# Late parts of the last attention block moved in a hand-written order, ahead of the first state-space block's norms, lengths and parameters

## The chip, the cores and the metric

One of the cores of one Trainium2 chip runs the whole network in one launch. The core has TensorE (PE in the profile; its weight loads are PEld), VectorE (DVE), ScalarE (ACT), GpSimd (POOL) and SyncE (SP), which here only issues DMAs. Each engine works through its own queue of instructions, and the queues wait for each other by semaphores. The metric is the device time of one execution, in microseconds, lower being better.

## The reference

The input `x` has 64 sequences of 64 positions with 256 channels; `cond` has 512 numbers for each sequence. Four layers follow, each added to its input:

```python
x = x + attention(x, cond)      # layer 0: 16 heads, width 256
x = x + attention(x, cond)      # layer 1
x = x + state_space(x, cond)    # layer 2: inner width 512, state 16
x = x + state_space(x, cond)    # layer 3

# attention: styled layer norm, then
q, k, v = (xn @ Wq.T) * q_dc, (xn @ Wk.T) * k_dc, (xn @ Wv.T) * v_dc * s2
out = softmax(q @ k.T * scale) @ v
return (out @ Ww.T) * w_dc + (v @ Wu.T) * u_dc

# state space: a gated recurrence over the 64 positions
xr, gate = split(x @ W_in.T);  xr = xr + cond
xc = silu(causal_conv4(xr) + b_conv)
xn = layernorm(xc) * ln_g + ln_b
Bm, Cm, dt = split(xn @ W_xproj.T)
dt = tanh(dt @ W_dt.T + b_dt) * 0.01
Ad = 1 - dt * tanh(A_log);  Bd = Bm * min(norm(xn), 1)
for t in range(64):
    h = clip(h * Ad[t] + Bd[t] * xn[t], -10, 10)
    y[t] = Cm[t] @ h + D * xn[t]
return (y * silu(gate)) @ W_out.T
```

All arithmetic is in float32.

## The kernel before

The activations stay in SBUF in one tile `xt`, channels on the partitions, from the first load to the last store. An attention block (`Att`) is 8 sequences, 512 columns, of one layer; there are 8 blocks for each of the two layers, 16 in all, so the last has index 15 and its tiles carry the name `1_7`. A state-space block (`Block`) is 32 sequences by 16 time steps of one layer; `b0`, `b1` and `b2` are the first three, all of layer 2 and of the same 32 sequences.

Each block is a set of small methods ("parts"), and each part issues a few instructions on one to three engines. The order of the parts is written by hand: a list of events with a due time each, which is sorted and then issued. An attention block's parts have times relative to its index (`att_plan`), so the parts of block 15 are due at 15 plus the table's number. The parts of `b0`, `b1` and `b2` that run beside the last attention block have absolute times, such as 15.63. Since almost all instructions are pinned to the order in which they are issued, a due time sets the place of a part in the queue of every engine that it uses. After the last event the loop over the time steps begins, and its order is another table.

These are the parts that matter, with the names that their tiles have in the profile.

Of the last attention block:

- `soft_a(g)`, `soft_b(g)` for four groups g: row maxima `mx` and subtraction `pr` on DVE, the exponential of `pr` on ACT, then sums `sm` on DVE and the product of `pr` with them on POOL (L816).
- `turn(g)`: PE transposes `pr` in two halves `pt`, and ACT copies each to `pT` (L830).
- `attend(g)`: PE multiplies `pT` with the values into `po`, for two groups at a time; `collect(h)`: ACT copies `po` to `oT` (L851).
- `out(3, oc)`: PE projects `oT` (`pw`), DVE scales it into `t` (L123).
- `add`: POOL adds the residual `xt` to the other projection, `t` (L865, 128x1024).
- `leave`: the sum goes back to `xt`; in the last block alone DVE adds one half (L123, `xt<-t,t`) and POOL the other (L880).

Of the state-space blocks:

- `project(c)`, `collect(c)` for four channel groups c: PE computes `acc`, DVE or ACT and POOL put it into the window `xr` (for `b0`, `b1` and the first group of `b2` it is one DVE addition, L123). `collect(0)` of a block first copies the halo of the block before (L195). All blocks use one `xr` buffer.
- `begin(c)` on ACT and `taps(c, 1, 2, 3)` on DVE (L117, `acc_s`): the first and the other three products of the convolution. The last tap of the last group is followed by the copy of the halo on POOL (L234).
- `silu(c)`: ACT, to `xc`.
- `turn_x(j)` for four row groups j: PE transposes `xc` to `ptr`; `stats(j)`: DVE computes mean and variance and the centred, scaled `xg`, POOL the inverse root `rs` (L301, L302). There are two `xg` buffers.
- `norm(j)`: ACT multiplies `xg` by `rs`, POOL adds the offset to give `xn` (L318).
- `length(j)`: ACT squares `xn` and sums (it writes over `xg`).
- `flip`, `flipped`: PE transposes the small projections to `pxt`, ACT copies them to `pt` (L277).
- `params`, `strength`, `by_step`, `spread_b`, `decay`, `spreads`: small POOL instructions on `pt` (L329 to L407, L348), with one ACT tanh; the last of them are `exa` and `exc` (L336).
- `turn_a`, `turned_a`, `turn_c`, `turned_c`: PE turns `exa` and `exc` to `pa` and `pc`, ACT copies them to `ad` and `cd`. POOL has cleared `cd` before (L975).
- The loop: for each time step PE computes the input product `pu`, DVE the clipped state `h` in two halves (L1069 at the first step, L1072 later), ACT the decayed state `v`, PE the output `py`.

PSUM tiles of the attention phase (`ptr`, `pt`, `pxt`, `acc`, `pw`) take turns in three buffers.

Of the kernel before, what the change touches and what calls it, by code (L numbers as in the profile page):

```python
# [60 lines left out]
def tile_kernel(ctx: ExitStack, tc: tile.TileContext, ins, out):  # L61
# [520 lines left out]
    with tc.tile_pool(name="xpool", bufs=1) as xpool, tc.tile_pool(  # L582
# [318 lines left out]
        ablocks = [Att(n) for n in range(len(atts))]  # L901
# [9 lines left out]
        b0, b1, b2 = blocks[0], blocks[1], blocks[2]  # L911
        events = []

        def at(when, *parts):
            events.extend((when, b, part, args) for b, part, *args in parts)

        for n, b in enumerate(ablocks):
            for when, *part in att_plan:
                at(n + when, (b, *part))

        for when, k in ((-0.83, 4), (-0.7, 4), (-0.45, 4), (0.05, 4), (0.7, 4)):
# [22 lines left out]
        at(15.38, *((b0, "silu", c) for c in range(IC)))  # L944
        at(15.409, (b0, "shared"), (b0, "keep"))
        at(15.47, (b0, "flip"), (b0, "flipped"))
        for j, when in enumerate((15.446, 15.49, 15.54, 15.624)):
            at(when, (b0, "turn_x", j), (b0, "stats", j), (b0, "norm", j, True), (b0, "length", j))
        at(15.61, (b1, "begin", 0), (b1, "begin", 1))
        at(15.63, (b0, "params"), (b0, "strength"), (b0, "by_step"), (b0, "spread_b", 0),  # L950
           (plan0, None), (b0, "decay"), (b0, "spreads"))
        at(15.64, (b1, "taps", 0, 1, 2, 3))
        at(15.8, (b1, "begin", 2), (b1, "begin", 3), (b1, "taps", 1, 1, 2, 3))
        at(15.9, (b1, "taps", 2, 1, 2, 3))
        at(16.071, (b2, "project", 0))
        at(16.1, (b1, "taps", 3, 1, 2, 3), (b2, "collect", 0))
# [9 lines left out]
    with tc.tile_pool(name="m1", bufs=1) as m1, tc.tile_pool(  # L966
# [95 lines left out]
        for n, blk in enumerate(blocks):  # L1062
            for t in range(BT):
                j, t4 = divmod(t, T4)
                hs = []
                for h in range(2):
# [3 lines left out]
                    else:  # L1070
                        pin(
                            nc.vector._custom_dve(  # L1072
                                TENSOR_ADD_SAT, out=hn, in0=vs[h], in1=pus[h], s0=10.0, s1=-10.0
# [107 lines left out]
```

## Time and profile before

| | us |
|---|---|
| runs shown (median; lowest to highest) | 1637.25; 1634.78 to 1639.84 |
| profiled execution, its own time | 1634.85 |
| its span | 1633.1 |
| around the span | 1.75 |
| first state update of the loop (DVE h L1069) begins | 579.62 into the span |

The profile is one execution of the program. Its page gives busy times for each engine, the span in 40 slices and the chain of work that ended last. A timeline lists an engine's instructions in order of time: start, duration, engine, line, operation, tiles (written `out<-in`), shapes, count, and in brackets the idle time ahead of it and what ended it. The granted TensorE clock was 0.99 over the span and lower in the stretch where attention hands over to the state-space layers (0.71 from 544 to 576).

### The profile page before, as it was taken

The page shows a single profiled execution, that of the slowest core. Times are in us where ns is not written, and L with a number is a line of the kernel's source. Part 1 is how long each engine was busy: PE and PEld are TensorE (multiplying, and loading weights), DVE is VectorE, ACT ScalarE, POOL GpSimd, SP SyncE. Part 2 cuts the span into 40 slices and gives each one's busy share as a digit, 9 for nine tenths or more (in the row PEclk, how much of TensorE's full clock was granted, in tenths as well). Part 3 has the DMA queues.
Part 4 walks back from the last instruction along what each step waited for, and adds up shares of the span by engine and source line. Part 5 has one row for each costly group of instructions (what it writes and reads, how often), then busy time and mean ns, then how long its engine had stood idle before and what let it go on. Part 6 is the DMA issues. An engine that isn't in the chain of part 4 may idle for free.

```text
span 1633.1 us, 30221 instructions
## 1 busy us (share of the span) xinstructions
PE 1541.5 (94%) x12352; PEld 640.1 (39%) x12352; DVE 1308.7 (80%) x1480; ACT 1117.4 (68%) x1899; POOL 867.3 (53%) x862
## 2 busy tenths in 40 slices
PE   5899999999999688999999999999999999999888
PEld 2555555555555322333333333333333333333223
DVE  3776777677776677998989888988898889888775
ACT  3555554454466467887878888878788887787774
POOL 2467566566666755365455464554554545635410
PEclk9999999999999799999999999999999999999999
DMA  7000000000000010000000000000000000000001
GB/s 236 2 1 2 2 2 2 2 2 2 2 2 2 1 62 1 1 1 1 1 1 1 1 1 1 1 1 1 1 8 7 14 1 14 14 1 14 14 1 27
DMA packets 19339, 18.27 MB, mean 11 GB/s; under 512 B 5473, under 2 KB 16353, under 8 KB 19201
## 3 DMA queue, kind: packets, MB, share of 16 engines
q1 hardware_dynamic: 19200, 16.34, 3.2%
q8 instruction: 98, 1.61, 0.4%
q14 instruction: 41, 0.33, 0.1%
HBM read 12.14 MB, written 4.19 MB: 10 GB/s over the span
## 4 chain that ended last, share of the span: by engine, by line
PE 73%; DVE 13%; ACT 8%; issue 3%; POOL 2%; DMA 1%; SPq 0%; DVEq 0%; POOLq 0%; ACTq 0%
PE pw L107 24%; PE pu L107 14%; DVE h L1072 11%; PE py L107 8%; ACT v L113 6%; PE acc L107 6%; PE pt L110 4%; PE pg L107 3%; PE pv L107 3%; PE ps L107 2%; PE po L107 2%; PE mx L107 2%; PE ptr L110 2%; POOL xr L204 1%; PE pm L107 1%
## 5 line engine op out<-in xcount | busy, mean ns | idle before, releaser
L113 ACT ACTIVATE v<-h,ad 128x512 f32<-128x512 f32 x1008 | 651.1, 710 | 116.0 <-DVE h L1072 111.3
L1072 DVE CUSTOM_DVE_ANT_0 h<-v,pu 128x1024 f32<-128x1024 f32 x504 | 593.1, 1217 | 126.4 <-PE pu L107 64.3
L107 PE MATMUL pu<-xn,bd 32*128 32x512 f32 x2048 | 293.7, 641 | 41.3 <-DVE h L1072 39.5
L204 POOL TENSOR_TENSOR xr<-xr,cT 128x512 f32<-128x512 f32 x55 | 70.3, 1278 | 401.4 <-ACT xr L203 401.4
L107 PE MATMUL py<-h,cd 128*32 128x512 f32 x2048 | 276.2, 610 | 0.5 <-DVE h L1072 0.4
L107 PE MATMUL pw<-xm,aw 128*128 128x512 f32 x384 | 179.9, 607 | 3.9 <-POOL xm L724 3.9
L107 PEld LDWEIGHTS pu<-xn,bd 32*128 32x128 f32 x2048 | 83.3, 183 | 210.7 <-issue 142.3
L816 POOL TENSOR_TENSOR pr<-pr,sm 128x1024 f32<-128x1024 f32 x64 | 121.1, 1902 | 21.9 <-DVE sm L815 20.4
L107 PE MATMUL pg<-xt,win 128*128 128x512 f32 x256 | 129.3, 607 | 2.9 <-ACT ad L113 2.9
L117 DVE SCALAR_TENSOR_TENSOR acc<-xr,cv,acc 128x512 f32<-128x512 f32 x165 | 123.9, 751 | 3.5 <-ACT acc L113 1.6
L107 PE MATMUL acc<-xt,win 128*128 128x512 f32 x256 | 123.8, 607 | 0.0
L830 ACT COPY pT<-pt 128x512 f32<-128x512 f32 x128 | 68.4, 586 | 76.1 <-PE pt L110 76.1
L107 PE MATMUL pw<-z,wo 128*128 128x512 f32 x240 | 119.0, 618 | 0.0
L107 PEld LDWEIGHTS py<-h,cd 128*32 128x32 f32 x2048 | 40.5, 108 | 196.9 <-issue 157.1
L113 ACT ACTIVATE pr<-pr 128x1024 f32<-128x1024 f32 x64 | 67.7, 1057 | 61.1 <-DVE pr L123 61.1
L107 PEld LDWEIGHTS pw<-xm,aw 128*128 128x128 f32 x384 | 69.0, 191 | 74.0 <-issue 65.3
L113 ACT ACTIVATE acc<-xr,cv 128x512 f32<-128x512 f32 x55 | 43.0, 782 | 77.3 <-POOL xr L204 77.3
L434 POOL TENSOR_TENSOR dx<-xn,rep 128x512 f32<-128x512 f32 x64 | 82.0, 1281 | 26.2 <-DVE ys L123 26.2
L805 DVE TENSOR_REDUCE mx<-ps 128x16 f32<-128x1024 f32 x64 | 78.3, 1223 | 13.7 <-PE ps L107 13.7
L712 POOL TENSOR_TENSOR sq<-sq 128x512 f32<-128x512 f32 x16 | 20.4, 1277 | 129.6 <-ACT sq L113 129.6
L318 POOL TENSOR_TENSOR xn<-xg,rep 128x512 f32<-128x512 f32 x64 | 82.0, 1282 | 8.0 <-ACT xg L113 3.3
L123 DVE TENSOR_TENSOR pr<-ps,mx 128x1024 f32<-128x1024 f32 x64 | 78.4, 1225 | 8.6 <-DVE mx L805 0.5
(144 smaller groups left out, 2298.4 us busy)
## 6 DMA issues: line engine op xcount, KB each, us to landing
xt<-in_xT SPq DMA_DIRECT2D x8, 512.0 KB, 7.8
out_xT<-xt SPq DMA_DIRECT2D x14, 256.0 KB, 2.3
aw<-in_aw SPq DMA_DIRECT2D x10, 256.0 KB, 6.2
win<-in_win SPq DMA_DIRECT2D x2, 1024.0 KB, 8.3
rep<-in_rep SPq DMA_DIRECT2D x2, 784.0 KB, 7.9
wo<-in_wo SPq DMA_DIRECT2D x2, 512.0 KB, 8.1
out_xT<-xt SPq DMA_DIRECT2D x2, 192.0 KB, 2.5
wx<-in_wx SPq DMA_DIRECT2D x2, 96.0 KB, 7.2
```

Source lines behind the costliest of these rows:

```text
L107: pin(nc.tensor.matmul(*args, **kw))
L110: pin(nc.tensor.transpose(*args))
L113: pin(nc.scalar.activation(*args, **kw))
L117: nc.vector.scalar_tensor_tensor(out=out, in0=in0, scalar=scalar, in1=in1, op0=op0, op1=op1)
L123: pin(nc.vector.tensor_tensor(*args))
L204: pin(nc.gpsimd.tensor_tensor(curb, curb, bc(temb, 2, BT), ALU.add))
L318: pin(nc.gpsimd.tensor_tensor(self.xn[j], xg, self.rep[:, DI : 2 * DI], ALU.add))
L434: pin(nc.gpsimd.tensor_tensor(self.dx[j], self.xn[j], self.rep[:, 2 * DI : 3 * DI], ALU.mult))
L805: pin(nc.vector.tensor_reduce(mx, s4, AX.X, ALU.max))
L816: pin(nc.gpsimd.tensor_tensor(pr, pr, bc(sm, 3, S), ALU.mult))
L830: pin(nc.scalar.copy(self.pT[g][:, c, :, :], pt))
L1072: nc.vector._custom_dve(TENSOR_ADD_SAT, out=hn, in0=vs[h], in1=pus[h], s0=10.0, s1=-10.0)
```

## The change

In the plan of the last attention block 13 parts get due times of their own, and the parts of the first state-space blocks around them are taken apart and set anew. `add` becomes later (15.454 to 15.7); the rest of the attention parts become earlier, the largest step being `leave` (16.44 to 15.73). For `b0`, `norm` and `length` are separated from `turn_x` and `stats`, so that the copies of `flipped` and `turn(1)` and the exponential of group 3 come ahead of `norm(0)` on ACT. What follows `params` moves from 15.63 to 15.67. `begin` and `taps` of `b1` are spread differently: the taps of group 1 stand between the last projection and `leave`, those of groups 2 and 3 after `leave`. No instruction is added or removed and no tile changes its size.

```diff
+        last_plan = {
+            ("add",): 0.7, ("attend", 0): 0.545, ("soft_b", 3): 0.605, ("turn", 2): 0.612,
+            ("attend", 1): 0.613, ("collect", 0): 0.614, ("turn", 3): 0.65, ("attend", 2): 0.651,
+            ("attend", 3): 0.652, ("collect", 1): 0.653, ("out", 3, 0): 0.71, ("out", 3, 1): 0.72,
+            ("leave",): 0.73,
+        }
         for n, b in enumerate(ablocks):
             for when, *part in att_plan:
+                if b is ablocks[-1]:
+                    when = last_plan.get(tuple(part), when)
                 at(n + when, (b, *part))
...
-        for j, when in enumerate((15.446, 15.49, 15.54, 15.624)):
-            at(when, (b0, "turn_x", j), (b0, "stats", j), (b0, "norm", j, True), (b0, "length", j))
-        at(15.61, (b1, "begin", 0), (b1, "begin", 1))
-        at(15.63, (b0, "params"), (b0, "strength"), (b0, "by_step"), (b0, "spread_b", 0),
+        for j, (x, norm, length) in enumerate((
+            (15.446, 15.484, 15.55), (15.49, 15.491, 15.552), (15.54, 15.551, 15.626), (15.62, 15.621, 15.66),
+        )):
+            at(x, (b0, "turn_x", j), (b0, "stats", j))
+            at(norm, (b0, "norm", j, True))
+            at(length, (b0, "length", j))
+        at(15.625, (b1, "begin", 0), (b1, "begin", 1))
+        at(15.63, (b0, "params"))
+        at(15.64, (b1, "taps", 0, 1, 2, 3))
+        at(15.67, (b0, "strength"), (b0, "by_step"), (b0, "spread_b", 0),
            (plan0, None), (b0, "decay"), (b0, "spreads"))
-        at(15.64, (b1, "taps", 0, 1, 2, 3))
-        at(15.8, (b1, "begin", 2), (b1, "begin", 3), (b1, "taps", 1, 1, 2, 3))
+        at(15.68, (b1, "begin", 2), (b1, "begin", 3))
+        at(15.725, (b1, "taps", 1, 1, 2, 3))
         at(15.9, (b1, "taps", 2, 1, 2, 3))
         at(16.071, (b2, "project", 0))
         at(16.1, (b1, "taps", 3, 1, 2, 3), (b2, "collect", 0))
```

The order that results on each engine, from the point where the two programs part to where they meet again, is this (parts of the attention block in capitals):

```text
ACT   flipped, TURN 1, EXP 3, norm 0, norm 1, length 0, norm 2, length 1, TURN 2, COLLECT 0,
      norm 3, begin b1 0 and 1, length 2, TURN 3, COLLECT 1, length 3, tanh, begin b1 2 and 3, silu b1
POOL  xn 0, rs 1, xn 1, PRODUCT 2, rs 2, xn 2, PRODUCT 3, rs 3, xn 3, params, strength, by_step,
      spread_b, decay, exa, exc, ADD, LEAVE, halo b1, xr b2, cd clear
DVE   stats 1, SUMS 2, xr b1 2, stats 2, SUMS 3, xr b1 3, stats 3, taps b1 0, OUT 3, taps b1 1,
      LEAVE, taps b1 2 and 3, xr b2 0, taps b2 0, first h
PE    turn_x 1, acc b1 2, turn_x 2, ATTEND 0, acc b1 3, TURN 2, ATTEND 1, turn_x 3, TURN 3,
      ATTEND 2 and 3, OUT 3, acc b2 0, pa, pc, pg, first pu
```

## The prediction

> **What bounds the kernel now.** I read the page first, then the chain of waits around the only stretch whose order changes, then each engine's timeline there. All times are us from the start of the span of the one profiled execution.
>
> ```profile
> PE 1541.5 (94%) x12352; PEld 640.1 (39%) x12352; DVE 1308.7 (80%) x1480; ACT 1117.4 (68%) x1899; POOL 867.3 (53%) x862
> PE 73%; DVE 13%; ACT 8%; issue 3%; POOL 2%; DMA 1%; SPq 0%; DVEq 0%; POOLq 0%; ACTq 0%
> ```
>
> Over the whole span TensorE bounds. That average says nothing about this change. Engine by engine, the two programs hold the same instructions, in the same order up to about 537 and again from the first state update on (DVE h L1069, 579.62); only the passage between differs. So the change is worth the shift of that first h, which every later step follows: no store or load moves, and the second layer's weight loads, issued from 577.61, land in about 8 us while their first user (PE pwx) runs at 613.51. What sets the first h is in the chain of waits:
>
> ```profile
> 570.50 0.59 ACT oT L851
> ...
> 571.13 3.70 PE pw L107 x8
> 574.84 0.81 PE pa L107 x8
> ...
> 575.88 0.81 ACT acc_s L113
> ...
> 576.72 1.42 DVE acc_s L117
> ...
> 579.62 2.35 DVE h L1069 x2
> ```
>
> The attention tail is last: oT is copied at 570.50, its projection pw ends at 574.84, pa follows on PE, ad on ACT waits for pa, the begin of block b2 stands behind ad on ACT, three taps follow, then h. The change pulls exactly this tail forward. The question is what ends last instead. VectorE:
>
> ```profile
> 554.83 5.87 DVE L117 SCALAR_TENSOR_TENSOR acc_s<-xr,cv,acc_s 128x512 f32<-128x512 f32 x6
> 564.39 6.96 DVE L117 SCALAR_TENSOR_TENSOR acc_s<-xr,cv,acc_s 128x512 f32<-128x512 f32 x6 [3.69 <-ACT acc_s L113]
> 572.32 0.69 DVE L123 TENSOR_TENSOR xr<-acc,cT 128x512 f32<-128x512 f32 x1 [0.96 <-POOL xr L195]
> 575.48 1.09 DVE L123 TENSOR_TENSOR xt<-t,t 128x512 f32<-128x512 f32 x1
> ```
>
> Block b1's twelve taps (6+6) were done at 571.35, before pw. GpSimd:
>
> ```profile
> 542.15 2.35 POOL L865 TENSOR_TENSOR t<-t,xt 128x1024 f32<-128x1024 f32 x1
> 567.96 1.38 POOL L336 TENSOR_TENSOR exa<-pt,const 128x512 f32<-128x512 f32 x1
> 569.30 1.50 POOL L336 TENSOR_TENSOR exc<-pt,const 128x512 f32<-128x512 f32 x1
> 571.77 0.51 POOL L195 COPY xr<-halo 128x384 f32<-128x384 f32 x1
> 575.65 1.94 POOL L880 TENSOR_TENSOR xt<-t,t 128x512 f32<-128x512 f32 x1 [3.37 <-DVE t L123]
> ```
>
> The residual add (L865) ran at 542.15, in a hole, and cost nothing. It is needed by leave (L123 xt on DVE, L880 on POOL). TensorE:
>
> ```profile
> 543.21 1.12 PE L110 MATMUL ptr<-const,xc 128*128 128x128 f32 x4 [4.16 <-ACT pt L277]
> 544.12 3.62 PE L107 MATMUL acc<-xt,win 128*128 128x512 f32 x4
> 549.16 1.98 PE L107 MATMUL acc<-xt,win 128*128 128x512 f32 x4
> 563.21 1.12 PE L110 MATMUL pt<-const,pr 128*128 128x128 f32 x4 [6.79 <-ACT pT L830]
> ```
>
> The two long holes (4.16 and 6.79) are ACT copies queued behind norms and lengths; the change fills them. After a hole the same four acc passes take 3.62 instead of 1.98.
>
> [...] pt's copy waited behind norm 0 and length 0 until 542.85 though pxt was there by 537.4. [...] taps took 746/880/1631 ns (min/median/max), the long one beside POOL xn. [...]
>
> **The change part by part.** No instruction is added or removed; no DMA moves. I walk the new queues with the durations above.
>
> 1. ACT copies pt and pT 1 ahead of norm 0. The PE hole of 4.16 goes: ptr 1 at 539.0, acc(b1,2) 539.1, ptr 2 541, attend 0, acc(b1,3) 542–544. But exp of pr 3 (operand ready 540.73, 1.07 long) is now ahead of norm 0: norm 0 moves from 540.13 to 541.6, and xn 0 from 540.93 to 542.3.
> 2. POOL's own chain mv, rs, xn, pr product remains serial, with ACT's norm between rs and xn. With xn 1 at 545.3 (547.08 before), pr 2 at 546.6 (548.30) and pr 3 at 551.7 (553.43) it gains 1.7, no more. There are two xg buffers, so stats 2 now waits for length 0 on ACT (0.9 idle on DVE, hidden by the wait for pr 2's product).
> 3. Tail: pt 2 at 548.6, oT's first copy at 552, pt 3 at 553.6; their copies stand behind norm 3, two begins and length 2 on ACT until 557.5–558.6; second oT copy 559.6–560.2; pw from 560.3, 3.7 long warm, 5.2 with a half-clock start: done 564–565.5. That is **9.4 to 10.8 earlier** than 574.84.
> 4. POOL: params follow xn 3 at 557; strength needs length 3, which ACT has at 560.1–560.8 behind the oT copy (0.2 idle). exc ends 568.0 [...], 569.9 if each row lasts as before (570.8). **Behind it stands add**: 2.35, so 570.4 to 572.3.
> 5. DVE waits there in leave: t (pw) at 563.8–566.1, b1's taps on channel 1 to about 569–571, then leave. [...] leave ends 571.5–573.4. **Behind leave in DVE's queue stand the six taps of channels 2 and 3**, which ran at 564.39–571.35. POOL has only the halo copy left, so they take 6 x 0.75 to 0.8 = 4.8 rather than 6.96: done 576.5–578.2, about 5 to 7 later than before.
> 6. Their end frees xr: POOL copy 0.5, DVE xr 0.69 (now 579.5 at the late end), ACT begin 0.80, three taps 2.25 to 2.98: 583.0–583.5.
> 7. PE's order is now pw, acc(b2,0), pa, pc; pc waits for xr of b2 (its bank), so PE idles from about 568 to 579.5 and restarts at half clock: pc 4 x 0.25, one pg pair 1.7, pu 1.44 (the row at 582.11) to 2.3: 583.7–584.6.
>
> **Sum.** PE's restart ends last in the late branch: h at 584.6 less 579.62, nearly +5.0; replaying step 5's taps at 6.96 instead gives 585.8 (+6.2) or, with every row as before, +6.7. I take **+5.3**. The profiled execution took 1634.85 (span 1633.1 and 1.75 around it), so 1640.15 for it; it lies 2.4 under the median shown, 1637.25, and I add the same to that: **1642.5**.
>
> Costed at nothing: the cd clear now follows xr's copy (578.9–580.7) and cd's copy ends at 581.3, under PE's restart; uncovered, it is the 1.48 that PE ptr waited for cd before. Two table loads stay two. The half-clock penalty that the loop's first iterations paid (py 1.94 at 583.48 against 1.06 at 590.68) may shrink since PE has run 5 us by then: 0 to -0.9; I take 0 because DVE's h there waits for ACT.
>
> **Rivals.** (a) Same mechanism, milder: [...] PE restarts fast. exc 567.5, add to 569.9, leave to 571, taps to 575.3, xr 576.6, pc to pu 4.1: h at 580.9, or 583.7 to 584.5 if PE restarts slowly but not all of step 7's late end comes. **+1.3 to +4.9**. For it: DVE is idle for 4 us before t, which lets POOL run free. Against: 11 us of PE idle have no warm counterpart in the trace. (b) **Not slower**: leave is never held, because POOL reaches add before DVE reaches leave. Place: POOL's queue; it decides if exc ends by about 564.7 (567.1 less 2.35). Then t is done at 564.8, taps of channel 1 567.1, leave 568.2, six taps 572.7, xr 574, begin 574.9, and PE restarts to 578.1: **-1.5**; with PE warm, -2.5 or a little more. Against: POOL was busy 10.70 of 11.50 us (559.9–571.4), so I see nothing there that shrinks by the 3.3 us from step 4's 568.0. (c) The moves could be undone by the buffers or by the scheduler; the built order shows them done.
>
> **How the numbers follow.** Main case 0.67, +4.9 (step 7's late end) to +7. (a) 0.25. (b) 0.08, with 0.05 of it for a gain over 0.3% should the loop also start warmer. About 0.3% (4.9 us) is what a measurement of this kernel tells from no change; the main case lies above it, narrowly at its lower end, and (a) inside it. Slower 0.67, same 0.28, faster 0.05. Range: (a)'s low end, 1638.5, with half a us for run scatter, to the main case's +7 and 1.7 scatter, 1646.
>
> **What would show it.** Right: ACT pt copy at about 537, pw ending by 566, POOL L865 starting at 567–570, DVE xt waiting for POOL t, six taps after it, a PE hole of some 11 us before pc, first h at 583.5–586. Wrong: h before 580, L865 done before DVE's t, or a gap that appears only after h.

## The result, and the profile after

| | before | after |
|---|---|---|
| runs of one comparison, median (lowest to highest; 8 each) | 1635.57 (1634.28 to 1639.84) | 1642.13 (1638.68 to 1642.76) |
| profiled execution, its own time | 1634.85 | 1642.76 |
| its span | 1633.1 | 1641.0 |

The changed kernel is slower: the ratio of the times is 1.0033, with a 95% interval from 1.0022 to 1.0045, which is 3.6 to 7.4 us. The page of the kernel after, busy times and the chain's shares by engine:

```profile
PE 1547.5 (94%) x12352; PEld 643.5 (39%) x12352; DVE 1308.9 (80%) x1480; ACT 1117.7 (68%) x1899; POOL 864.8 (53%) x862
PE 72%; DVE 13%; ACT 8%; issue 3%; POOL 2%; DMA 1%; SPq 0%; DVEq 0%; POOLq 0%; ACTq 0%
```

The counts are those of before. PE's busy time grew by 6.0 us with the same 12352 matmuls, so some of them ran slower; not all of that is the change.

**First, where the two executions part.** The two profiled executions differ by 7.91 us. A timeline of PE shows that nearly half of it was there long before the first moved instruction. Kernel before, about 28 us into the span:

```profile
28.47 7.09 PE L107 MATMUL pw<-xm,aw 128*128 128x512 f32 x16
```

Kernel after, the same matmuls:

```profile
29.54 9.66 PE L107 MATMUL pw<-xm,aw 128*128 128x512 f32 x16
```

Sixteen passes of an identical program took 9.66 instead of 7.09. In the kernel after the first six took 5.16, 0.86 each, and the other ten 4.50, 0.45 each; before, all sixteen ran at 0.44. So the first six ran at about half the rate. (The granted clock of this trace doesn't show it, as it reads 1.00 for those six; it shows a second stretch at 0.50, from 44.95 to 48.36.) Together with the matmuls around them the later execution is 3.74 behind when block 14's projection starts on PE, the last thing ahead of the changed order: at 535.97 instead of 532.23. This is scatter of single executions: in the runs below, whose programs are the same up to there, that start lies between 532.23 and 534.86. From here on I measure **the passage**: from the start of block 14's pw to the start of the first h. It took 47.39 before (579.62 less 532.23) and takes 51.30 after (587.28 less 535.97): **+3.92** (differences are taken before rounding). The loop, from the first h to the last pair of them, took 1040.29 and takes 1040.53: +0.24. So the two differ by 4.16 from the passage on; 3.74 of the 7.91 is not the change's doing. The 0.24 may not be either: in the runs below, where the loop is the same program, it took from 1039.1 to 1041.6.

**The chain of waits after**, in the passage (start, length, engine and tile):

```profile
563.17 5.41 PE pw L107 x8
...
568.61 0.69 DVE t L123
569.30 1.45 DVE acc_s L117
...
570.77 2.72 DVE acc_s L117
...
573.52 1.65 DVE acc_s L117
575.16 1.30 DVE xt L123
576.46 0.57 DVE acc_s L117
...
580.99 0.51 POOL xr L195
...
582.37 1.09 PE pc L110 x4
583.46 1.71 PE pg L107 x2
585.16 2.09 PE pu L107 x8
...
587.28 2.36 DVE h L1084 x2
```

Before, the chain went from oT through pw and ad to the first tap of b2. Now it leaves PE after pw and stays on DVE for 12 us, in block b1's taps and leave, and then goes through xr back to PE, which has idled for 11.29. DVE's own timeline of the kernel after:

```profile
569.21 5.95 DVE L117 SCALAR_TENSOR_TENSOR acc_s<-xr,cv,acc_s 128x512 f32<-128x512 f32 x3
575.09 1.37 DVE L123 TENSOR_TENSOR xt<-t,t 128x512 f32<-128x512 f32 x1
576.31 4.53 DVE L117 SCALAR_TENSOR_TENSOR acc_s<-xr,cv,acc_s 128x512 f32<-128x512 f32 x6
```

Three taps of group 1 took 5.95, the six after leave only 4.53. What ran beside the three is in POOL's timeline of the kernel after:

```profile
569.13 1.05 POOL L336 TENSOR_TENSOR exc<-pt,const 128x512 f32<-128x512 f32 x1
570.14 2.79 POOL L865 TENSOR_TENSOR t<-t,xt 128x1024 f32<-128x1024 f32 x1
573.01 1.61 POOL L880 TENSOR_TENSOR xt<-t,t 128x512 f32<-128x512 f32 x1
```

The tap of 2.72 runs beside add (L865) and ends 0.56 behind it, the tap of 1.65 in the same way beside POOL's half of leave (L880). Note that DVE's leave has no idle time ahead of it: DVE never stands waiting for add, it loses the same time in taps that last up to three and a half times their 0.75. And PE's timeline of the kernel after:

```profile
542.62 0.60 PE L110 MATMUL ptr<-const,xc 128*128 128x128 f32 x4
543.06 1.88 PE L107 MATMUL acc<-xt,win 128*128 128x512 f32 x4
...
582.37 1.09 PE L110 MATMUL pc<-const,exc 128*128 128x128 f32 x4 [11.29 <-DVE xr L123]
583.25 1.92 PE L107 MATMUL pg<-xt,win 128*128 128x512 f32 x2
585.09 2.09 PE L107 MATMUL pu<-xn,bd 32*128 32x512 f32 x8
```

The hole of 4.16 ahead of ptr is gone, as the change meant; a hole of 11.29 stands ahead of pc in its place, and what follows it takes 1.92 and 2.09 where it took 1.02 and 1.14 before (PE pg at 576.55, pu at 577.50). The granted clock over pc, pg and pu was 0.50 after and 1.00 before. Below, "half clock" and "cold" stand for pg and pu at these 1.92 and 2.09, "warm" for 1.02 and 1.14.

### The profile page after: what moved, and what is told of

It reads as the page before. It is cut to its first block, busy times and chain, and to the rows that moved or that the text cites. A ratio compares the mean times of both kernels' runs of the same rounds, so it can differ in the third digit from the quotient of the medians.

```text
span 1641.0 us, 30226 instructions
## 1 busy us (share of the span) xinstructions
PE 1547.5 (94%) x12352; PEld 643.5 (39%) x12352; DVE 1308.9 (80%) x1480; ACT 1117.7 (68%) x1899; POOL 864.8 (53%) x862
## 4 chain that ended last, share of the span: by engine, by line
PE 72%; DVE 13%; ACT 8%; issue 3%; POOL 2%; DMA 1%; SPq 0%; DVEq 0%; POOLq 0%; ACTq 0%
PE pw L107 24%; PE pu L107 14%; DVE h L1087 11%; PE py L107 8%; ACT v L113 6%; PE acc L107 5%; PE pt L110 4%; PE pg L107 3%; PE pv L107 3%; PE ps L107 2%; PE po L107 2%; PE mx L107 2%; PE ptr L110 2%; POOL xr L204 1%; PE pm L107 1%
```

## The experiments

Three theories were to be told apart. **A**: add and leave, late on POOL and DVE, hold nine taps of b1 (three beside add, six behind leave), and these now end last. **B**: PE's cold restart after the long hole is what costs; the taps alone would not. **C**: the first half of the chain is to blame, that is the new order of norms, lengths and parameters. Each experiment is judged by the passage of its own profiled execution, since single times carry the early scatter of up to 3.7 us and the scatter of the loop. There is one profiled execution of each kernel, so a gain of the passage by one or two us is not shown as a gain of the whole time: the loop behind it took from 1039.1 (nine filling calls) to 1041.6 (leave last), for 1040.5 in the kernel after, and whether that is scatter alone isn't shown. The edits are against the kernel after, except in the two that do one half of the change alone.

**Add back in its early hole.**

```diff
-            ("add",): 0.7, ("attend", 0): 0.545, ("soft_b", 3): 0.605, ("turn", 2): 0.612,
+            ("attend", 0): 0.545, ("soft_b", 3): 0.605, ("turn", 2): 0.612,
```

> The changed kernel, with the residual add back at its old due time (15.454), ahead of xn 0 on POOL. I compare the passage from the start of the projection pw of block 14 to the first h: 47.4 us before, 51.3 after. Theory A (leave waits for add behind exc, and six taps stand behind leave on DVE): leave no longer waits for POOL, the passage is 49.2, about 2 less than after; it does not fall to 47.4, since the begin of groups 2 and 3 and the taps of group 1 still come late and TensorE still restarts after a hole of 9 us. Theory B (the loss is TensorE's restart at half clock alone): the hole stays over 8 us, so 51.3 stays within 0.5. Theory C (the loss is the later norm 0 and the later state-space parts): 51.3 or more, since add now delays xn 0.

Passage **49.59**, 1.71 shorter (one time of 1638.0). DVE's timeline of this run:

```profile
566.67 3.33 DVE L117 SCALAR_TENSOR_TENSOR acc_s<-xr,cv,acc_s 128x512 f32<-128x512 f32 x3
569.92 1.07 DVE L123 TENSOR_TENSOR xt<-t,t 128x512 f32<-128x512 f32 x1
570.84 4.54 DVE L117 SCALAR_TENSOR_TENSOR acc_s<-xr,cv,acc_s 128x512 f32<-128x512 f32 x6
```

The three taps of group 1 fall from 5.95 to 3.33; POOL did add at 540.06 in 2.38, where it costs nothing. But the passage is still 2.2 above that of before, so late add is a part of the loss and not all of it. PE restarted at half clock here too (pg 1.92, pu 2.09), while b2's third tap had ended on DVE at 580.04. Were PE warm, h could start there, 47.8 into the passage; that is an estimate from this trace, and no run had both.

**Leave behind the taps**, with add still late.

```diff
-            ("leave",): 0.73,
+            ("leave",): 1.2,
```

> The changed kernel with add left at its late place, but leave moved from 15.73 to 16.2, behind the six taps of groups 2 and 3 and behind the window of b2 on DVE. Theory A: the taps no longer stand behind a waiting instruction, the passage (47.4 before, 51.3 after) is 49.2, as with the early add. Theory B: 51.3. Theory C: 51.3.

Passage **49.66**, 1.64 shorter (1640.26). DVE's timeline of this run:

```profile
568.58 8.63 DVE L117 SCALAR_TENSOR_TENSOR acc_s<-xr,cv,acc_s 128x512 f32<-128x512 f32 x9
...
578.51 1.56 DVE L123 TENSOR_TENSOR xt<-t,t 128x512 f32<-128x512 f32 x1
```

Nine taps in one piece, with add still late: 8.63, where the kernel after needs 11.6 from its first tap to its last (569.21 to 580.84), leave included. Taking either one out of the taps' way gives about the same. Both runs end in the same half-clock restart (pg 1.91 and pu 2.09 here).

**POOL given 2.4 us more ahead of add**: in the last block `add` first multiplies its tile by one, a further POOL pass of the same size, whose values stay as they are.

```diff
+                if self is ablocks[-1]:
+                    t4 = self.pp[4].rearrange("p c t -> p (c t)")
+                    pin(nc.gpsimd.tensor_tensor(t4, t4, one.broadcast_to([P, HC * TB]), ALU.mult))
```

> The changed kernel with one more POOL instruction of 128x1024 right ahead of the late add (the tile times one, so no value changes), about 2 us long. Theory A: leave, the six taps and the first h move by the same 1.9 to 2.1, the passage is 53.3. Theory B: the restart costs the same wherever it lies, but it lies behind xr, so the passage grows only if DVE's taps do: B has no number of its own here below 51.3 and above 51.8. Theory C: 51.3, since norms and lengths are untouched.

Passage **53.53**, 2.23 longer (1641.09). POOL's timeline of this run:

```profile
566.99 2.40 POOL L867 TENSOR_TENSOR t<-t,one 128x1024 f32<-128x1024 f32 x1
569.47 2.66 POOL L868 TENSOR_TENSOR t<-t,xt 128x1024 f32<-128x1024 f32 x1
```

Of the 2.40 added to POOL there, 2.23 reach the first h. That is A's claim in its sharpest form: POOL's work between exc and leave is on the path, nearly one for one. PE's restart behind it took the same as in the kernel after (1.09, 1.92 and 2.09).

**PE kept busy through the hole** with matmuls whose result nobody reads, behind `turn_a`; first 9 calls, then 11. A call shows as two passes in the profile.

```diff
+        def busy(self, ps, n):
+            for _ in range(n):
+                mm(ps[:, 0, :, :, :], ones_h, xt[:, 0, 0:TB], start=True, stop=True)
...
+        at(16.455, (b0, "busy", ps, 9))
```

> The changed kernel with nine matmuls of 128x512 without a use, into the score bank that nobody reads any more, between pa and pc on TensorE: they fill most of the 11.29 us hole and end before pc's bank is free. Theory A with the restart as its last term: pc, pg and pu run at full clock (2.5 instead of 4.9), then the taps of b2 bound (their end lay 1.8 ahead of h), the passage is 49.5. Theory B: the whole loss goes, 47.4 or near. If the half clock did not matter: 51.3.

Passage **50.76** (1637.51). The expectation was missed, and PE's timeline of this run says why:

```profile
568.86 7.97 PE L107 MATMUL ps<-xt,ones_h 128*128 128x512 f32 x18
579.14 0.72 PE L110 MATMUL pc<-const,exc 128*128 128x128 f32 x4 [2.31 <-DVE xr L123]
579.65 1.92 PE L107 MATMUL pg<-xt,win 128*128 128x512 f32 x2
581.50 1.84 PE L107 MATMUL pu<-xn,bd 32*128 32x512 f32 x8
```

The filling ended 2.31 before pc could start, and pg and pu ran at half clock all the same (1.92 and 1.84). So 11 calls were used:

> As e4_pe_filled, with eleven unused matmuls instead of nine, so that they end some 0.5 before pc instead of 2.3. There the passage was 50.8, with pg and pu still at half clock. If the half clock of pc, pg and pu is the last term of the sum, they now take about 2.6 together, the taps of b2 bound, and the passage is 49.5. If the gap of 2.3 was not what kept the clock low: 50.8 again.

Passage **49.52**, 1.78 shorter (1640.54). PE's timeline of this run:

```profile
571.00 9.69 PE L107 MATMUL ps<-xt,ones_h 128*128 128x512 f32 x22
581.28 0.63 PE L110 MATMUL pc<-const,exc 128*128 128x128 f32 x4 [0.59 <-DVE xr L123]
581.74 1.02 PE L107 MATMUL pg<-xt,win 128*128 128x512 f32 x2
582.70 1.14 PE L107 MATMUL pu<-xn,bd 32*128 32x512 f32 x8
```

With a gap of only 0.59, pc, pg and pu take what they took before, and pu ends at 583.84. The first h starts at 584.33, straight behind b2's third tap on DVE. So the restart costs 1.8 on the path, and no more can be had from PE: the DVE chain is right behind it. B is a part, too: with PE warm the passage is still 2.1 above that of before.

Up to pc the two filled runs repeat the kernel after, and they show what the taps wait for. Their pw, 6.72 long in the run with 9 calls, ended 1.2 later in the passage than in the kernel after, where it took 5.40; yet pc began at 46.46 and 46.47, where it began at 46.39. So pw, which stands in the chain of the page, is nearly tied there with POOL's add and leave. POOL's timeline of the run with 11 calls (exc, add, POOL's half of leave):

```profile
567.86 1.05 POOL L336 TENSOR_TENSOR exc<-pt,const 128x512 f32<-128x512 f32 x1
568.87 2.35 POOL L869 TENSOR_TENSOR t<-t,xt 128x1024 f32<-128x1024 f32 x1
571.30 1.61 POOL L884 TENSOR_TENSOR xt<-t,t 128x512 f32<-128x512 f32 x1
```

The first tap of group 1 came 0.4 behind the start of add there, and the three taps took 5.08, for 3.33 with add early.

**The attention block's new times alone**, in the kernel before (`last_plan` added, the state-space events as they were).

> The kernel before with the first half of the change alone: the last attention block's 13 due times, the state-space parts where they were. Passage from pw of block 14 to the first h: 47.4 before, 51.3 after. Theory A: add still stands behind exc, which now comes later since norms and lengths hold up ACT as before, and leave comes ahead of more taps: 52.8. Theory C (the loss is in the state-space half of the change): 47.4 or less.

Passage **53.98**, 6.6 above before (1642.02). DVE's timeline of this run:

```profile
568.17 0.69 DVE L123 TENSOR_TENSOR t<-pw,dc 128x512 f32<-128x512 f32 x1 [10.88 <-PE pw L107]
...
571.97 7.89 DVE L117 SCALAR_TENSOR_TENSOR acc_s<-xr,cv,acc_s 128x512 f32<-128x512 f32 x9
```

Here DVE idles 10.88 for pw with all nine taps of groups 1 to 3 queued behind out and leave. In the kernel before all twelve were done (571.35) ahead of t. Add is not what holds them here: it ended at 570.16, before pw did at 570.41. The passage was 1.2 longer than expected.

**The state-space half alone**, in the kernel before.

> The kernel before with the second half of the change alone: norms, lengths, what follows params, begins and taps moved, the attention block's parts with add at their old times. Theory A: the late attention tail still ends last, as before, and nothing waits for add: 47.0, 0.4 less than before at most. Theory C: 51 or more.

Passage **46.50**, 0.9 *below* before (1635.15). PE's timeline of this run:

```profile
570.50 3.70 PE L107 MATMUL pw<-oT,aw 128*128 128x512 f32 x8 [0.72 <-ACT oT L851]
574.04 0.96 PE L107 MATMUL pa<-const,exa 128*128 128x16 f32 x8
575.45 0.63 PE L110 MATMUL pc<-const,exc 128*128 128x128 f32 x4 [0.45 <-ACT ad L113]
```

Here pw starts 38.02 after block 14's pw (570.50 less 532.48), where before it was 38.90. The tail comes 0.9 earlier, which is more than the 0.4 expected; PE has no long hole ahead of pc, and the taps remain ahead of the tail. C falls: the new order of norms and lengths by itself does no harm. The halves alone give +6.6 and -0.9 and together +3.9, so they don't simply add: the second half makes the tail early, which takes back part of what the first one costs.

**A version built from this**: the tail early as in the kernel after, but add back in its hole, the fourth `turn_x` a little earlier, all twelve taps of b1 ahead of out, and leave last.

```diff
-            ("add",): 0.7, ("attend", 0): 0.545, ("soft_b", 3): 0.605, ("turn", 2): 0.612,
+            ("add",): 0.483, ("attend", 0): 0.545, ("soft_b", 3): 0.605, ("turn", 2): 0.612,
...
-            ("leave",): 0.73,
+            ("leave",): 1.2,
...
-            (15.446, 15.484, 15.55), (15.49, 15.491, 15.552), (15.54, 15.551, 15.626), (15.62, 15.621, 15.66),
+            (15.446, 15.484, 15.55), (15.49, 15.491, 15.552), (15.54, 15.551, 15.626), (15.604, 15.621, 15.66),
...
-        at(15.625, (b1, "begin", 0), (b1, "begin", 1))
+        at(15.625, *((b1, "begin", c) for c in range(IC)))
...
-        at(15.68, (b1, "begin", 2), (b1, "begin", 3))
-        at(15.725, (b1, "taps", 1, 1, 2, 3))
-        at(15.9, (b1, "taps", 2, 1, 2, 3))
+        at(15.641, (b1, "taps", 1, 1, 2, 3))
+        at(15.642, (b1, "taps", 2, 1, 2, 3))
         at(16.071, (b2, "project", 0))
-        at(16.1, (b1, "taps", 3, 1, 2, 3), (b2, "collect", 0))
+        at(15.643, (b1, "taps", 3, 1, 2, 3))
+        at(16.1, (b2, "collect", 0))
```

> A version put together from what theory A says: the changed kernel with add at 15.483, in POOL's hole ahead of xn 0; all four begins of b1 ahead of the last transposes, and all twelve taps of b1 on DVE ahead of out and leave; leave last (16.2); turn_x and stats of row group 3 a little earlier (15.604). Theory A: DVE's taps fill its holes, xr and pc come 8 earlier than after, the passage is 43 to 44.5, that is 3 to 4.4 less than before, 0.2 to 0.3% of the whole. Theory B: TensorE's hole and its restart remain, 49 or more. Theory C: with the late norm 0 kept, 49 or more.

Passage **43.77**, 3.6 below before and 7.5 below after. The median of 6 runs is 1633.19 (1631.55 to 1635.4) against 1637.89 for the 10 runs of the kernel before beside it: a ratio of 0.997, interval 0.9956 to 0.9984, faster by 2.6 to 7.2 us. DVE's timeline of this run:

```profile
558.14 11.52 DVE L117 SCALAR_TENSOR_TENSOR acc_s<-xr,cv,acc_s 128x512 f32<-128x512 f32 x12 [1.91 <-ACT acc_s L113]
569.58 1.27 DVE L123 TENSOR_TENSOR t<-pw,dc 128x512 f32<-128x512 f32 x2
572.82 0.69 DVE L123 TENSOR_TENSOR xr<-acc,cT 128x512 f32<-128x512 f32 x1 [1.96 <-POOL xr L195]
```

Twelve taps run in one piece while PE computes the tail, and t follows at once. The window xr waits 1.96 for POOL's copy of the halo, which stands behind exc (exc ended at 572.33), so ahead of PE's restart it is now POOL's own work that ends last. PE starts pc at 573.65 and still pays for a cold restart: pg took 1.91 and pu 2.09. The moves of this version weren't tried one by one, so what each is worth isn't shown.

## Why the prediction was right, and where its sum was off

The forecast was 1642.5, slower for the likeliest case; the median is 1642.13. The direction stands, and so does the mechanism in the main: the tail came 10.0 earlier, and add, leave, six taps and PE's restart end last in its place. How add delays DVE was wrong (step 5). That the number fits so well is partly luck. The forecast put 5.3 on the median of the three runs shown, 1637.25; with all eight runs beside this result it is 1635.57, 1.7 less, and the medians differ by 6.6, 1.3 more than 5.3, so two misses nearly cancel. And in the pair of profiles the passage and the loop cost 4.16 where the sum had 5.3, while the slow passes early in the span add 3.74 that no step had. Below, times of the kernel after are put into the frame of before by taking off 3.74.

- **Step 1 was right.** ptr ran at 538.9 for 539.0, its hole gone, and acc took 1.88.
- **Step 2 was right.** xn 1 ran at 545.5 for 545.3, the product of group 2 at 546.7 for 546.6 and that of group 3 at 551.5 for 551.7, and DVE waited 0.97 for length 0, for 0.9.
- **Step 3 was right.** pw ended at 564.8, 10.0 earlier, for 9.4 to 10.8. It took 5.40 at a granted clock of 0.68, the half-clock start that the step had at 5.2; in the run with nine filling calls, the same program up to there, it took 6.72.
- **Step 4 was mis-sized by 1.6 to 3.5.** exc ended at 566.4 for 568.0 to 569.9. exa and exc took 1.05 each, where the kernel before had 1.38 and 1.50: DVE ran no tap beside exa (it was idle, then scaled pw), and beside exc it was DVE's first tap that took longer (1.45 for 0.75). add followed at once, as said, but took 2.79 for 2.35, and ended at 569.2 for 570.4 to 572.3.
- **Step 5 was right in its times and not in how they come about.** leave ended at 572.7 for 571.5 to 573.4, and the six taps took 4.53 for 4.8, ending at 577.1. But the step had DVE standing in leave until add is done, and said that the trace would show xt waiting for t. It showed three taps of 5.95 instead (1.45, 2.72 and 1.65), ending at 571.4, where the step had them end at about 569 to 571 and DVE stand from then on; leave followed them without a gap. Without add beside them they took 3.33 (add in its early hole). The trace of before had a sign of it, a tap of 1.63 that began 0.22 behind POOL's xn at 557.93 and ended 0.54 behind it, where the shortest took 0.75; the step made the six later taps shorter because POOL would have little left to do, and did not reckon with add beside the three.
- **Step 6** had xr done at 579.5 at its late end; it was done at 578.5, 1.0 earlier, since the taps ended 1.1 ahead of their late end.
- **Step 7 was right in kind.** PE restarted at 578.6 after 11.29 of idle (for "some 11"), and pc, pg and pu took 1.09, 1.71 and 2.09: 4.9 in all, near the late end of the step, which comes to 5.0. That pu ended at 583.5, by the step's early end of 583.7, is owed to the earlier xr and not to a quick restart. Half clock is shown by the granted clock (0.50 over pc, pg and pu) and by the two filled runs: warm, the three take 2.6 together and the passage gets 1.78 shorter.
- **The sum was off in two terms.** Its +5.0 starts from xr at 579.5; with xr at 578.5 the same restart gives +4.0, and +3.92 came. And it moved on to +5.3 for dearer taps (+6.2, +6.7), where the six took 4.53. So the passage itself ended below the main case (from +4.9) and within the range of rival (a) (+1.3 to +4.9): exc came even earlier than (a) had it (566.4 for 567.5), and PE restarted as the main case had it. Rival (a)'s upper part doesn't follow from its own steps, though: its xr at 576.6 with a slow restart of 5.0 gives 581.6, +2.0. The 583.7 it names is step 7's, from an xr at 579.5.
- **Costed at nothing.** The clear of cd ended at 583.2 in the profile of after, 4 us ahead of the first h, and held nothing. The loop was to gain 0 to 0.9 from a warmer PE and took 0.24 more, well inside its scatter.

Rival (b) needed exc by 564.7; it came at 566.4, 1.7 too late. Its reason came true in form, since leave itself was not held; but only because the taps ahead of leave had paid for add. Rival (c) was excluded by the trace, which shows the new order.

What stays open: the medians differ by 6.6, and the ratio's interval is 3.6 to 7.4, where this pair of profiles has 4.16 for the change. The rest can be those slow early passes, which with what is around them put the start of the passage between 532.2 and 536.0 in ten profiled executions, or the loop (1039.1 to 1041.6 in the same ten). The median of the kernel before itself was 1635.57 over the 8 runs beside this result and 1637.89 over the 10 beside the version above. But only one execution of the kernel after has a trace, so how its other seven started isn't shown.

## What to carry to other kernels

When the last step of a chain is pulled forward, write down for each queue what now stands behind it: here nine short vector instructions that had filled a wait were put behind the tail's projection, six of them behind its transfer back too, and they became the tail. A long GpSimd pass moved beside VectorE work can cost that work nearly its own length, even if nobody waits for it by a semaphore (three taps took 5.95 beside an add of 2.79 and 3.33 without it, and of 2.40 more on POOL 2.23 reached the first h), so leave it in the hole where it was; the taps first, add early and leave last turned a passage 3.9 longer into one 3.6 shorter, with the other attention parts where the change had put them. And before two profiled executions are subtracted, find the last instant at which their programs are equal and see how far apart they already are.

## What was not expected of the hardware

- The same instructions of the same program took 7.09 in one execution and 9.66 in another, early in the span; the first six of sixteen passes took 0.86 each in the slower one, the others 0.45. It moved everything after it by up to 3.7 us, as much as the change did.
- After a gap of 2.31 behind 8 us of uninterrupted full passes, the next large matmuls ran at half clock (pg 1.92 for two passes; the small pc ahead of them hardly slowed, 0.72 for 0.63). After a gap of 0.59 pg took 1.02. From the last filling pass to pg it was 2.82 in the one run and 1.05 in the other, with pc in between. That is one execution of each, and no gap between the two was tried.
- Of add and a tap that ran beside each other, the one that began later took longer. In the run with 11 filling calls the first tap came 0.4 behind the start of add: add took 2.35, as in its hole (2.35 and 2.38), and the three taps 5.08 for 3.33. In the kernel after a tap was under way when add began: there add took 2.79, and the next tap, begun 0.63 behind it, 2.72 for 0.75.
